# A four-layer graph attention kernel: row tiles 4-7 of layer 1 and row tile 24 of layers 2 and 3 change between gathered and all-node attention

## The chip, the cores and the metric

The kernel runs on one core of a Trainium2 chip, as one launch. The metric is the device time of a launch in microseconds, as the median of several runs; lower is better. PE is TensorE, DVE is VectorE, ACT is ScalarE, POOL is GpSimd and SP is the engine whose queue issues most plain transfers.

## What is computed

Four graph attention layers run one after the other on 4096 nodes with 256 features. Each layer is followed by a residual sum and a layer norm. All layers use one adjacency matrix; a node has itself and about 16 others as neighbours.

```
_a = bernoulli(key, 0.00390625, (4096, 4096)) | eye(4096)       # adj
...
# layer 1 (layer 0 is of the same form)
Wh = einsum('nf,hfo->hno', x, W)                      # 4 heads of 64
s1, s2 = einsum('hno,ho->hn', Wh, a1), einsum('hno,ho->hn', Wh, a2)
e = leaky_relu(s1[:, :, None] + s2[:, None, :], 0.2)
e = where(adj[None] > 0, e, NEG_BIG)
att = softmax(e, axis=-1)
h_prime = einsum('hij,hjo->hio', att, Wh)
...
x = layernorm(x + gnn(x, adj, ...))
```

Layer 2 has two heads of 128. Layer 3 has one score per pair, used once with each sign, with 256 values for each, and an ELU at its end.

## The kernel before

Nodes are taken in 32 row tiles of 128. A layer has a table of values in DRAM (`vals`): a row per node, with the head's values, each scaled, and the node's scores. For every row tile a layer computes the weighted sum over neighbours in one of two ways.

A **gathered** row tile (`RowTile`) reads only nodes that some row of the tile needs. A list of places (`idx`), made in layer 0, names for each tile 13 sets of 128 table rows; GpSimd issues an indirect transfer for each (L797), and one more set, the tile's own rows, is a plain load. The 14 sets are worked on in two halves: `half(0)` needs 6 gathers, which name only rows of tiles below 23 (`MIX`), and `half(1)` needs 7, which may name any row. In each half ACT computes exponentials set by set (L907 in layers 0 to 2, L874 in layer 3), DVE masks them (L864, L909, L876, L878), and PE multiplies by the gathered values (L928). In layers 0 and 1, three of the four heads come from ACT as the exponential of a sum of two scores (`LOGS` = 3), and the fourth from DVE as a product of two stored exponentials (`EXPS` = 1; L898 and L903). Buffers for gathered rows (`g0`, `g1`) hold four tiles.

An **all-node** row tile belongs to a group of four row tiles (`WHOLE`, by blocks of four). For each of the 32 column tiles `j` a step loads the table's values (`vw`), spreads packed mask bits into bytes (`bytes`, L660 mw), makes the weights (`pw`) and multiplies. Layers 2 and 3 do this in `whole_rows` (L1200 to L1211), where ACT and DVE make the weights and PE takes one matmul per row tile and head. Layer 1 does it in `whole_heads` (L1239 to L1290), where DVE alone makes them from exponentials held in `Sw` and `cw` (L1269), two heads in each of two passes over the 32 column tiles; PE takes eight matmuls per step, four of one form (L1272) and four of another (L1274). Every f32 matmul is two records in the trace.

Layer 0 has no all-node group. Layer 1 has block 7 (row tiles 28-31), so 28 gathered tiles. Layer 2 has blocks 3, 7 and 6, so 20. Layer 3 has blocks 7 and 6, so 24. Gathered tiles run in ascending order (`ORDER`).

The order of work is that of the program: each engine takes its own instructions in order. `steps` runs over the gathered tiles' halves; `half_with_whole` issues a half and then as many all-node steps as `whole` allows, so that all of them are spread evenly and end three tiles before the last. Finished tiles are normed (`finish`, `norm`, in groups by `GROUPS`), stored, and projected into the next layer's table by `Projection` (L677 to L742). `close` joins two layers: it loads the next layer's first tiles, projects what is left, and, from a layer that has all-node groups, runs ten steps of the next layer's groups early.

The lines that carry the two layouts are these.

```
LOGS = (3, 3, 2, 1)
EXPS = (1, 1, 0, 0)
...
WHOLE = ((), (7,), (3, 7, 6), (7, 6))
AHEAD = 10
ORDER = tuple([m for m in range(NT) if m // BT not in w] for w in WHOLE)
```

Of the kernel before, what the change touches and what calls it, by code (L numbers as in the profile page):

```python
# [37 lines left out]
F32 = mybir.dt.float32  # L38
# [3 lines left out]
I32 = mybir.dt.int32  # L42
# [8 lines left out]
P = 128  # L51
# [4 lines left out]
BT = 4  # L56
# [24 lines left out]
PAIRS = (tuple(range(1, 1 + FIRST)), tuple(range(NPAIR - FIRST)))  # L81
GROUPS = (((24, 4),), ((24, 2), (28, 1), (31, 2)), ((16, 2), (17, 1), (20, 2), (24, 1), (31, 2)), ((24, 1), (31, 4)))
LEAD = 4
# [15 lines left out]

LOGS = (3, 3, 2, 1)  # L100
EXPS = (1, 1, 0, 0)
TERMS = tuple(a + b for a, b in zip(LOGS, EXPS))
# [11 lines left out]

WHOLE = ((), (7,), (3, 7, 6), (7, 6))
AHEAD = 10
ORDER = tuple([m for m in range(NT) if m // BT not in w] for w in WHOLE)

# [8 lines left out]
def kernel(ctx: ExitStack, tc: tile.TileContext, ins: dict, out: bass.AP):  # L127
# [12 lines left out]
        "shift30": const.tile([P, 1], F32, name="shift30"),  # L140
        "shift3": const.tile([4, 4], F32, name="shift3"),
        "zero": const.tile([4, 4], F32, name="zero"),
# [14 lines left out]
    nc.vector.memset(shared["shift3"], -2.0 * KEXP)  # L157
    nc.gpsimd.affine_select(out=shared["shift3"], in_=shared["shift3"], pattern=[[1, 4]], compare_op=ALU.is_gt,
                            fill=0.0, base=0, channel_multiplier=-1)
# [24 lines left out]
class Program:  # L184
# [99 lines left out]
    def lists(self, ctx):  # L284
# [94 lines left out]
        class Block:  # L379
# [21 lines left out]
            def squeeze(self, part):  # L401
                js = slice(part * JG, (part + 1) * JG)
                src = self.mk.rearrange("p j t c -> p (j t c)").bitcast(I32) \
                    .rearrange("p (j t c) -> p j t c", j=JG, t=BT)
                w = P // 4
                for k in (4, 2, 1):
                    w //= 2
                    dst = self.bits[:, js] if k == 1 else wk.tile([P, JG, BT, w], I32, name=f"fold{k}", bufs=1)
                    nc.vector.scalar_tensor_tensor(dst, src[:, :, :, w:], k, src[:, :, :, :w],
                                                   op0=ALU.logical_shift_left, op1=ALU.bitwise_or)  # L410
                    src = dst
                if part == BT - 1:
                    rows = shared["v"][0][self.blk % 2][:N, :BW].rearrange("(j p) w -> p j w", p=P)
                    nc.sync.dma_start(out=rows, in_=self.bits.rearrange("p j t w -> p j (t w)").bitcast(F32))
                    if any(self.blk in w for w in WHOLE):
                        nc.sync.dma_start(out=shared["bitsW"][self.blk], in_=self.bits)
# [189 lines left out]
    def run(self):  # L606
# [40 lines left out]
        self.bk, self.vp, self.dp = self.pool("bk", 1), self.pool("vp", 6), self.pool("dp", 8)  # L647
        self.mwp, self.mup, self.mkp = self.pool("mwp", 2), self.pool("mup", 6), self.pool("mkp", 3)
        for n in (1, 2, 3):
# [107 lines left out]
class RowTile:  # L757
# [77 lines left out]
    def half(self, half):  # L835
# [21 lines left out]
        w = [pair[:, k, :U] for pair in pairs for k in range(2)]  # L857
        if n < 2:
            w = [w[1], w[2], w[3], w[0]]
# [20 lines left out]
        else:  # L880
# [23 lines left out]
            for h in range(A):  # L904
                for u in range(U):
                    for rows, g in parts[u]:
                        nc.scalar.activation(w[h][:, u, rows], S[:, h, rows], AF.Exp, bias=d(g, h))  # L907
                if n == 2:
                    nc.vector.scalar_tensor_tensor(w[h], w[h], LEAST, mh, op0=ALU.max, op1=ALU.mult)  # L909
                elif h % 2 == 0:  # L910
                    last = masked(pairs[h // 2])
            if n == 0:
                with self.layer.prog.tc.issue_after(last.ins):
                    nc.vector.tensor_scalar(self.kept(half), self.came(half), 0, None, op0=ALU.bitwise_or)
            turns = ((3, 0), (1, 2)) if n < 2 else ((0,), (1,))

# [38 lines left out]
class Layer:  # L955
# [3 lines left out]
    def __init__(self, prog, n):  # L959
# [5 lines left out]
        self.units = self.whole_rows() if n >= 2 else self.whole_heads()  # L965
        self.total = len(WHOLE[n]) * NT * (1 if n == 2 else 2)
        self.used = self.ahead = 0
# [200 lines left out]
    def whole_rows(self):  # L1168
        n, nc, prog, sh = self.n, self.nc, self.prog, self.shared
        H, Wd, T = HEADS[n], WIDTH[n], TERMS[n]  # L1170
        groups = [range(H)] if n < 3 else [(0,), (1,)]
        for blk in WHOLE[n]:
            tiles = range(blk * BT, (blk + 1) * BT)
            S = prog.bk.tile([P, T, BT, P], F32, name="Sw")
            for it, m in enumerate(tiles):
                nc.sync.dma_start(out=S[:, :, it, :], in_=sh["e"][n][m].partition_broadcast(P))
            bits = self.block_bits(blk)
            zs = [None] * BT
            for heads in groups:
                accs = [prog.bank(prog.pfour) for _ in range(BT)]  # L1180
                c0, c1 = heads[0] * Wd, (heads[-1] + 1) * Wd
# [10 lines left out]
                for j in range(NT):  # L1192
# [3 lines left out]
                    for h in heads:  # L1196
                        p = prog.dp.tile([P, BT, P], F32, name="pw")
                        d = sh["d"][n][:, j, h if n < 3 else 0:h + 1 if n < 3 else 1]
                        if n < 3:
                            nc.scalar.activation(p, S[:, h], AF.Exp, bias=d)  # L1200
                            nc.vector.scalar_tensor_tensor(p, p, LEAST, mj, op0=ALU.max, op1=ALU.mult)  # L1201
                        else:
                            nc.scalar.activation(p, S[:, 0], AF.Relu, bias=d)  # L1203
                            if h == 0:
# [4 lines left out]
                        c = h * Wd - c0  # L1209
                        for it in range(BT):  # L1210
                            nc.tensor.matmul(accs[it][:, c:c + Wd], p[:, it, :], v[:, c:c + Wd],  # L1211
                                             start=(j == 0 and h == heads[0]), stop=(j == NT - 1),
                                             skip_group_check=True)
                    if n == 3 and heads[0] == 0 and j == NT - 1:
                        def between(accs=accs):
                            for it in range(BT):
                                zs[it], last = self.positive(accs[it], whole=True)
                            return last
# [8 lines left out]
    def whole_heads(self):  # L1227
# [6 lines left out]
        nc.vector.tensor_scalar(c, c, HUGE, TINY, op0=ALU.min, op1=ALU.max)  # L1234
        for blk in WHOLE[n]:
            tiles = range(blk * BT, (blk + 1) * BT)
            S = prog.bk.tile([P, T, BT, P], F32, name="Sw")
            for it, m in enumerate(tiles):
                nc.sync.dma_start(out=S[:, :, it, :], in_=sh["e"][n][m].partition_broadcast(P))  # L1239


            for h in range(A):
                nc.scalar.activation(S[:, h], S[:, h], AF.Exp, scale=-1.0, bias=sh["shift30"])
                nc.vector.tensor_scalar(S[:, h], S[:, h], HUGE, None, op0=ALU.min)
            for h in range(A, T):
                nc.vector.reciprocal(S[:, h], S[:, h])
                nc.vector.tensor_scalar(S[:, h], S[:, h], LEAST, HUGE, op0=ALU.mult, op1=ALU.min)
            bits = self.block_bits(blk)
            z = prog.bk.tile([P, BT, H, Wd], F32, name="zh")
            for up, flat in TWOS:  # L1250
# [11 lines left out]
                for j in range(NT):  # L1262
# [4 lines left out]
                    for h in (up, flat):  # L1267
                        p[h] = prog.dp.tile([P, BT, P], F32, name="pw")
                        nc.vector.scalar_tensor_tensor(p[h], S[:, h], c[:, j, h:h + 1], mj, op0=ALU.max, op1=ALU.mult)  # L1269
                    how = dict(stop=j == NT - 1, skip_group_check=True)  # L1270
                    for it in range(BT):
                        nc.tensor.matmul(bu[:, it * Wd:(it + 1) * Wd], p[up][:, it, :],  # L1272
                                         v[:, up * Wd:(up + 1) * Wd], start=j == 0 and it == 0, **how)
                        nc.tensor.matmul(bf[:Wd, it * P:(it + 1) * P], v[:, flat * Wd:(flat + 1) * Wd],  # L1274
                                         p[flat][:, it, :], start=j == 0 and it == 0, **how)
                    yield
                nc.scalar.copy(z[:, :, up, :], bu[:, :BT * Wd].rearrange("p (t c) -> p t c", t=BT))
                turned = prog.bk.tile([Wd, BT, P], F32, name="turned")
                nc.scalar.copy(turned, bf[:Wd, :].rearrange("p (t i) -> p t i", t=BT))
                self.set_banks()  # L1280
                bt = prog.bank(prog.banks)
                for it in range(BT):
                    nc.tensor.transpose(bt[:, it * Wd:(it + 1) * Wd], turned[:, it, :], sh["ident"][:Wd, :Wd])
                nc.scalar.copy(z[:, :, flat, :], bt[:, :BT * Wd].rearrange("p (t c) -> p t c", t=BT))
            for it, m in enumerate(tiles):
                self.finish(m, z[:, it].rearrange("p h c -> p (h c)"), self.load_x(m), None)

    def block_bits(self, blk):
        bits = self.prog.mwp.tile([P, NT, BT, MW], I32, name="bw")
        self.nc.sync.dma_start(out=bits, in_=self.shared["bitsW"][blk])  # L1290
        return bits

    def bytes(self, bits, j):
        mj = self.prog.mup.tile([P, BT, P // 4], I32, name="mw")
        spread(self.nc, mj, bits[:, j], self.shared["pat"])
        return mj.rearrange("p t i -> p (t i)").bitcast(U8).rearrange("p (t i) -> p t i", t=BT)

# [547 lines left out]
```

## Time and profile before

| | |
|---|---|
| median of 3 runs | 2787.8 us (2785.93 to 2805.77) |
| the profiled execution's own time | 2012.93 us |
| its span | 2011.1 us |
| mean granted TensorE clock | 0.936 |
| HBM traffic | 401.51 MB read, 48.81 MB written |

The profile describes one execution, which took less time than the runs that were only timed. The span falls into stages. Up to about 100 us the first nodes are projected and the lists begun. Gathers of layer 0 start at 97.2 us, of layer 1 at 641.8, of layer 2 at 1121.0 and of layer 3 at 1533.2. Multiplication by gathered values follows its gathers by some tens of microseconds: PE works on layer 1 from about 705 to 1143 us. In a row of the groups view, the first number after the bar is the group's total busy time, the second the mean duration of one instruction in ns, and after the second bar stands the idle time of the engine ahead of the group.

### The profile page before, as it was taken

Reading aid. Unit: us, or ns where it says so; the run is one execution under the profiler, and the core shown is the slowest. Engines: PE = TensorE matmul, PEld = TensorE weight load, DVE = VectorE, ACT = ScalarE, POOL = GpSimd, SP = SyncE. Lnnn points to the kernel's source line nnn. Section 1 sums busy time; section 2 is a strip of 40 time slices with the busy share of each in tenths; the row PEclk is TensorE's granted clock in tenths of the full one; section 3 lists DMA queues with packets and bytes.
Section 4 is the critical chain, followed back from the end, with each engine's and each line's share of the span. In section 5 each row is a group of like instructions: output and inputs, shape, how many; then the busy total and the mean of one; then the engine's idle time right before and its main releaser. Section 6 shows DMA issues by size and latency. Waiting matters only on the chain.

```text
span 2011.1 us, 46792 instructions
## 1 busy us (share of the span) xinstructions
PE 1796.4 (89%) x15281; PEld 1481.6 (74%) x15281; DVE 1551.8 (77%) x5095; ACT 1498.1 (74%) x4659; POOL 1391.5 (69%) x1387
## 2 busy tenths in 40 slices
PE   5758889988999699998998989999998899899995
PEld 3537777777778589887886788898886677577773
DVE  3458988888889599988887877888876576676765
ACT  4559999898878577877666788877774687676863
POOL 0067777777777777777777677777753777767772
PEclk7758999999899799999999999999999999999998
DMA  8799999989767766666656656667666888888883
GB/s 292 227 336 325 319 298 286 293 293 296 217 170 203 200 177 190 180 182 178 179 167 183 194 158 189 199 189 203 184 187 188 248 266 247 266 251 251 258 250 105
DMA packets 291947, 453.59 MB, mean 226 GB/s; under 512 B 90246, under 2 KB 206059, under 8 KB 291692
## 3 DMA queue, kind: packets, MB, share of 16 engines
q0 software_dynamic: 74880, 227.83, 38.7%
q1 hardware_dynamic: 212194, 218.46, 35.0%
q10 hardware_dynamic: 4618, 4.20, 0.6%
q8 instruction: 123, 2.02, 0.4%
q14 instruction: 132, 1.08, 0.2%
HBM read 401.51 MB, written 48.81 MB: 224 GB/s over the span
## 4 chain that ended last, share of the span: by engine, by line
PE 46%; DMA 14%; ACT 12%; POOL 10%; DVE 9%; issue 6%; SPq 1%; DVEq 0%; ACTq 0%; POOLq 0%
PE bank L928 22%; PE bank L1211 12%; POOL G L797 10%; DMA G<-vals,idx 8%; ACT w L907 7%; PE bank L691 5%; DVE w L864 3%; DMA raw<-in_adjB_dram 2%; PE bank L1274 2%; ACT mk L399 1%; ACT pw L1200 1%; PE bank L1272 1%; DMA G<-vals 1%; PE bank L522 1%; PE bank L524 1%
## 5 line engine op out<-in xcount | busy, mean ns | idle before, releaser
L797 POOL DMA_INDIRECT G<-vals,idx x1352 | 1386.0, 1025 | 587.9 <-issue 350.0
L928 PE MATMUL bank<-G,w 128*64 128x130 f32 (+5 forms) x9156 | 920.8, 304 | 72.7 <-DVE w L864 60.7
L907 ACT ACTIVATE w<-S,G 128x64 f32<-128x64 f32 (+1 forms) x3080 | 824.3, 351 | 125.3 <-DMA G<-vals,idx 116.2
L928 PEld LDWEIGHTS bank<-G,w 128*64 128x64 f32 (+1 forms) x9156 | 741.4, 156 | 232.1 <-DVE w L864 76.5
L1211 PE MATMUL bank<-vw,pw 128*128 128x129 f32 (+1 forms) x2560 | 419.4, 322 | 13.7 <-issue 6.3
L1211 PEld LDWEIGHTS bank<-vw,pw 128*128 128x128 f32 x2560 | 375.1, 194 | 53.8 <-issue 17.7
L864 DVE SCALAR_TENSOR_TENSOR w<-w,bank 128x1024 f32<-128x1024 f32 (+1 forms) x240 | 322.7, 1345 | 10.2 <-ACT w L907 8.7
L691 PE MATMUL bank<-wext,xT 128*128 128x268 f32 (+3 forms) x640 | 185.6, 424 | 16.2 <-ACT xT L682 14.9
L874 ACT ACTIVATE w<-S,G 128x64 f32<-128x64 f32 (+1 forms) x329 | 104.1, 352 | 72.1 <-DMA G<-vals,idx 48.7
L691 PEld LDWEIGHTS bank<-wext,xT 128*128 128x128 f32 x640 | 121.4, 207 | 40.8 <-ACT xT L682 17.7
L1200 ACT ACTIVATE pw<-Sw,d 128x512 f32<-128x512 f32 x192 | 134.3, 711 | 21.0 <-PE bank L1211 12.5
L1201 DVE SCALAR_TENSOR_TENSOR pw<-pw,mw 128x512 f32<-128x512 f32 x192 | 129.5, 686 | 26.2 <-ACT pw L1200 25.1
L399 ACT ACTIVATE mk<-raw 128x1024 uint8<-128x1024 int32 x128 | 129.6, 1049 | 21.1 <-DMA raw<-in_adjB_dram 21.0
L1208 DVE TENSOR_TENSOR pw<-pw,mw 128x512 f32<-128x512 f32 x128 | 87.9, 689 | 63.1 <-ACT pw L1205 38.3
L903 DVE TENSOR_TENSOR w<-S,G 128x384 f32<-128x384 f32 x180 | 91.1, 509 | 41.8 <-DMA G<-vals,idx 36.2
L1203 ACT ACTIVATE pw<-Sw,d 128x512 f32<-128x512 f32 x128 | 89.7, 709 | 27.2 <-PE bank L928 10.4
L1272 PE MATMUL bank<-vw,pw 128*128 128x65 f32 x512 | 89.7, 258 | 17.5 <-DVE pw L1269 17.5
L1274 PE MATMUL bank<-pw,vw 128*65 128x128 f32 x512 | 99.7, 278 | 0.0
L1272 PEld LDWEIGHTS bank<-vw,pw 128*128 128x128 f32 x512 | 78.7, 195 | 26.2 <-issue 24.8
L1269 DVE SCALAR_TENSOR_TENSOR pw<-Sw,cw,mw 128x512 f32<-128x512 f32 x128 | 92.8, 740 | 0.0
L682 ACT COPY xT<-bank 128x256 f32<-128x256 f32 x128 | 45.7, 359 | 58.2 <-PE bank L677 37.9
L660 DVE TENSOR_TENSOR mw<-bw,pat 128x128 int32<-128x128 int32 x288 | 80.6, 285 | 1.6
(197 smaller groups left out, 1893.6 us busy)
## 6 DMA issues: line engine op xcount, KB each, us to landing
raw<-in_adjB_dram SPq DMA_DIRECT2D x128, 512.0 KB
G<-vals,idx POOLq DMA_INDIRECT x1352
vw<-vals SPq DMA_DIRECT2D x128, 128.5 KB
S<-edge SPq DMA_DIRECT2D x60, 256.0 KB
vw<-vals SPq DMA_DIRECT2D x96, 129.0 KB
xp<-y SPq DMA_DIRECT2D x96, 128.0 KB
y<-xp SPq DMA_DIRECT2D x96, 128.0 KB
vals<-row SPq DMA_DIRECT2D x64, 152.0 KB
```

The costliest lines, as they stand in the source:

```text
L399: nc.scalar.activation(self.mk[:, 2 * q:2 * q + 2], src, AF.Copy)
L691: nc.tensor.matmul(pp[:, :c1 - c0], self.xT[:, k, :], wext[:, k, c0:c1], start=(k == 0), stop=(k == KT - 1 and brow is None))
L797: nc.gpsimd.indirect_dma_start(out=self.row(half, k), out_offset=None, in_=self.values[:N + 1 if half else MIX * P, :].rearrange("r (k c) ...
L864: return nc.vector.scalar_tensor_tensor(pair, pair, LEAST, mh2, op0=ALU.max, op1=ALU.mult)
L874: nc.scalar.activation(w[0][:, u, rows], S[:, 0, rows], AF.Relu, bias=d(g, 0))
L907: nc.scalar.activation(w[h][:, u, rows], S[:, h, rows], AF.Exp, bias=d(g, h))
L928: nc.tensor.matmul(a, w[h][:, u, rows], b, start=half == 0 and u == 0 and (n == 3 or h == turns[0][0]), stop=half == 1, skip_group_check=True)
L1200: nc.scalar.activation(p, S[:, h], AF.Exp, bias=d)
L1201: nc.vector.scalar_tensor_tensor(p, p, LEAST, mj, op0=ALU.max, op1=ALU.mult)
L1211: nc.tensor.matmul(accs[it][:, c:c + Wd], p[:, it, :], v[:, c:c + Wd], start=(j == 0 and h == heads[0]), stop=(j == NT - 1), skip_group_ch ...
L1272: nc.tensor.matmul(bu[:, it * Wd:(it + 1) * Wd], p[up][:, it, :], v[:, up * Wd:(up + 1) * Wd], start=j == 0 and it == 0, **how)
L1274: nc.tensor.matmul(bf[:Wd, it * P:(it + 1) * P], v[:, flat * Wd:(flat + 1) * Wd], p[flat][:, it, :], start=j == 0 and it == 0, **how)
```

## The change

Layer 1 gets a second all-node group, row tiles 4-7, ahead of 28-31, so 24 tiles are gathered. Its fourth head is now an exponential of a sum from ACT as well, in gathered and all-node tiles alike (`LOGS` = 4, `EXPS` = 0). Groups are given as ranges of row tiles rather than blocks, and may have fewer than four. In layers 2 and 3 the last group becomes row tiles 25-27; row tile 24 is gathered (21 and 25 gathered tiles).

In `whole_heads` the score rows of the next group are loaded at step 8 and prepared at step 24 of the last pass over the group before, in a second `Sw` buffer. Each finish of a tile gets a turn of its own (a `yield`), with the tile's residual loaded one ahead. Gathered halves of layer 1 mask heads (0, 1) and (2, 3) in pairs after the second of a pair, and multiply in that order. The pool of mask bytes (`mup`) has five buffers instead of six, and the norm's groups follow the new last groups.

```
-GROUPS = (((24, 4),), ((24, 2), (28, 1), (31, 2)), ((16, 2), (17, 1), (20, 2), (24, 1), (31, 2)), ((24, 1), (31, 4)))
+GROUPS = (((24, 4),), ((24, 2), (28, 1), (31, 2)), ((16, 2), (17, 1), (20, 2), (25, 1), (31, 2)), ((25, 1), (28, 3), (31, 4)))
...
-LOGS = (3, 3, 2, 1)
-EXPS = (1, 1, 0, 0)
+LOGS = (3, 4, 2, 1)
+EXPS = (1, 0, 0, 0)
...
-WHOLE = ((), (7,), (3, 7, 6), (7, 6))
+WHOLE = (
+    (),
+    (range(4, 8), range(28, 32),),
+    (range(12, 16), range(28, 32), range(25, 28),),
+    (range(28, 32), range(25, 28),),
+)
...
-        self.mwp, self.mup, self.mkp = self.pool("mwp", 2), self.pool("mup", 6), self.pool("mkp", 3)
+        self.mwp, self.mup, self.mkp = self.pool("mwp", 2), self.pool("mup", 5), self.pool("mkp", 3)
...
-        if n < 2:
+        if n < 2 and A < T:
             w = [w[1], w[2], w[3], w[0]]
...
-                elif h % 2 == 0:
+                elif h % 2 == (A == T):
                     last = masked(pairs[h // 2])
...
-            turns = ((3, 0), (1, 2)) if n < 2 else ((0,), (1,))
+            turns = ((0,), (1,)) if n == 2 else ((0, 1), (2, 3)) if A == T else ((3, 0), (1, 2))
...
-        self.total = len(WHOLE[n]) * NT * (1 if n == 2 else 2)
+        self.total = len(WHOLE[n]) * NT * (1 if n == 2 else 2) + (sum(map(len, WHOLE[n])) if n < 2 else 0)
...
-        for blk in WHOLE[n]:
-            tiles = range(blk * BT, (blk + 1) * BT)
-            S = prog.bk.tile([P, T, BT, P], F32, name="Sw")
+        def scores(tiles):
+            S = prog.bk.tile([P, T, BT, P], F32, name="Sw", bufs=2)[:, :, :len(tiles)]
             for it, m in enumerate(tiles):
                 nc.sync.dma_start(out=S[:, :, it, :], in_=sh["e"][n][m].partition_broadcast(P))
+            return S
+        def floors(S):
             for h in range(A):
                 nc.scalar.activation(S[:, h], S[:, h], AF.Exp, scale=-1.0, bias=sh["shift30"])
                 nc.vector.tensor_scalar(S[:, h], S[:, h], HUGE, None, op0=ALU.min)
...
+        later = scores(WHOLE[n][0])
+        floors(later)
+        for q, tiles in enumerate(WHOLE[n]):
+            g, S = len(tiles), later
...
+                    if up == TWOS[-1][0] and q + 1 < len(WHOLE[n]):
+                        if j == JG:
+                            later = scores(WHOLE[n][q + 1])
+                        if j == 3 * JG:
+                            floors(later)
                     yield
...
+            y = self.load_x(tiles[0])
             for it, m in enumerate(tiles):
-                self.finish(m, z[:, it].rearrange("p h c -> p (h c)"), self.load_x(m), None)
+                yield
+                self.finish(m, z[:, it].rearrange("p h c -> p (h c)"), y, None)
+                if it + 1 < g:
+                    y = self.load_x(m + 1)
```

Counted over the program, from before to after: indirect gathers 1352 to 1326 (layer 1: 364 to 312; layer 2: 260 to 273; layer 3: 312 to 325); all-node steps in layer 1 64 to 128; L1211 matmuls 768 to 704 in layer 2 and 512 to 448 in layer 3; L907 exponentials 3080 to 3276; L903 and L898 together 240 to 128.

## The prediction

> **What bounds the kernel now.** I read the busy shares first, then the forty slices, then the costliest groups, then busy time by stage, then the waits and the order of time inside one stage.
>
> ```profile
> PE 1796.4 (89%) x15281; PEld 1481.6 (74%) x15281; DVE 1551.8 (77%) x5095; ACT 1498.1 (74%) x4659; POOL 1391.5 (69%) x1387
> ...
> PE   5758889988999699998998989999998899899995
> ...
> POOL 0067777777777777777777677777753777767772
> ...
> L797 POOL DMA_INDIRECT G<-vals,idx x1352 | 1386.0, 1025 | 587.9 <-issue 350.0
> L928 PE MATMUL bank<-G,w 128*64 128x130 f32 (+5 forms) x9156 | 920.8, 304 | 72.7 <-DVE w L864 60.7
> ```
>
> POOL's 7s are not slack. Of its 587.9 us idle, 350.0 are the 0.30 us between one gather and the next ("issue"). The waits of POOL leave little else: 91.7 us before the first gather, 7.5, 2.4 and 5.4 us, and this one:
>
> ```profile
> POOL G L797 <- ACT row L711: 42.2, 1, 42.2
> ```
>
> So from 132 to 1491 us gathers run back to back. Counting starts (416, 364, 260, 312 gathers for layers 0 to 3), layer 1's queue runs from 641.8 to 1121.0 us: 479.2/364 = 1.316 us a gather. Layer 2's last 236 run from 1156.3 to 1491.0: 1.418 us each. Only in layer 3 does POOL wait repeatedly, for L928 to give buffers back.
>
> Busy time by stage (span, then PE, weight load, DVE, ACT, POOL; last clock, DMA):
>
> ```profile
> 705.00:1143.00 438.00, 410.43 (x4269) 359.02 (x4264) 383.29 (x1125) 323.77 (x1241) 336.84 (x333) 0.98 0.64 181
> 1143.00:1491.00 348.00, 321.76 (x2790) 297.89 (x2789) 284.71 (x936) 273.37 (x785) 269.12 (x243) 0.97 0.66 189
> ...
> 1540.00:1960.00 420.00, 400.82 (x2135) 297.23 (x2135) 285.94 (x1020) 308.60 (x694) 304.03 (x295) 0.97 0.84 254
> ```
>
> The reader sees PE at 94, 92 and 95% in layers 1, 2 and 3. Layers 1 and 2 are held by the gather queue with PE a few per cent behind it; layer 3 is held by PE. PE's own work is read from starts, where it runs without a gap:
>
> ```profile
> 720.42 4.16 PE L928 MATMUL bank<-G,w 128*128 128x130 f32 x56
> 724.41 0.33 PE L1272 MATMUL bank<-vw,pw 128*128 128x65 f32 x2
> ...
> 725.98 4.97 PE L928 MATMUL bank<-G,w 128*128 128x130 f32 x56
> 730.78 0.33 PE L1272 MATMUL bank<-vw,pw 128*128 128x65 f32 x2
> ...
> 1159.74 8.32 PE L1211 MATMUL bank<-vw,pw 128*128 128x129 f32 x73
> ...
> 1668.42 5.36 PE L1211 MATMUL bank<-vw,pw 128*128 128x257 f32 x24
> 1673.62 4.13 PE L928 MATMUL bank<-G,w 128*128 128x257 f32 x28
> ```
>
> A layer-1 gathered half takes 724.41-720.42 = 4.0 us and the other 730.78-725.98 = 4.8: 8.8 us a row tile. Between them one all-node step (16 records) takes 725.98-724.41 = 1.57 us. L1211 costs 0.112 us a record in layer 2 (start to next start, 8.15/73) and 0.217 in layer 3 (5.20/24). Gathered tiles cost 4.7 us in layer 2 (28 records 2.13 to 2.57) and 8.75 in layer 3.
>
> **What the Trainium skill says.** "Perfetto Trace Analysis", section "Identifying the Most-Contended Engine", calls matmul busy share a bad measure because matmuls are pipelined. The trace agrees: mean L928 is 304 ns, but starts are 71 to 86 ns apart; hence prices by starts. "TensorE: Matmul & The Clock Gate", "Back-to-back issue gap", gives N/2.4+2.5 ns, 56 ns at 129 columns; the 112 ns measured for these f32 records is twice that, so the trace's price is used. The same page, "HAM oscillation", says idle gaps bring the clock down: from 680 to 700 us PE was busy 4.96 of 20 us at a clock of 0.51. A steadier PE could regain a little.
>
> **The change, part by part.**
>
> *Layer 1, tiles 4-7 to all nodes.* Gathers: 4 x 13 = 52 fewer, 52 x 1.316 = 68 us less POOL. PE: minus 4 x 8.8 = 35, plus 64 steps x 1.57 = 100: **+65 us**. DVE: two L1269 (92.8/128 = 0.725 effective) and one mask spread (80.6/288 = 0.28) a step, 64 x 1.73 = +111; four gathered tiles less, each four L864 (322.7/60 = 5.4) and unpacking (about 1.1), -26. ACT: 4 x 42 exponentials less at the effective 0.27 us (824.3/3080), -45. SP: 64 more L1258 loads of 130 KB, four score rows and one mask block in place of four tiles' loads and 52 gathers of about 137 KB; bytes balance within 2 MB at a DMA share of 0.64. One more mask block (256 KB) is stored in layer 0, under 1 us at its 300 GB/s, beside other work. The eight yields and the scores fetched eight steps into a pass hide behind matmuls; were that cover gone, one late score row costs about 4 us (Sw waits elsewhere reach 4.5).
>
> *Fourth head from ScalarE.* In 24 tiles, 14 more exponentials each: 24 x 14 x 0.27 = +91 us ACT. DVE loses L903 (three) and L898 (one), about 1.8 us a tile: -51 over the old 28. Layer-1 totals on the 705-1143 base: PE 410+65 = 475, DVE 383+111-26-51 = 417, ACT 324-45+91 = 370 and ten small ones more, POOL 312 x 1.316 = 411. ACT and DVE stay under PE, so I cost the head itself at nothing; the cover is PE's 475. Without it DVE at 417 would be late next. L903 also held DVE's queue while gathers landed (28.8 us between 900 and 1100), blocking L1269 behind it; that wait goes with a queue that no longer bounds.
>
> PE thus becomes layer 1's bound. It starts at 705 either way, so the stage ends no earlier than 705+475 = 1180, against 1143: **+37** with no idle left, +65 if all 27.6 us of idle stay. I take **+45**. POOL will now wait for buffers, as in layer 3, and does not carry its lead into layer 2: layer 2's second-half gathers need every layer-1 result.
>
> *Layer 2, tile 24 gathered.* POOL +13 x 1.418 = +18. PE minus 128 records x 0.112 = 14.3, plus 4.7 = -10. ACT: 28 exponentials more (+8), 64 all-node ones shorter by a quarter (0.711 us to about 0.60: -7). DVE: 64 x (0.14+0.07) less, 4 more maskings of 0.75: -10. The gather queue bounds here: **+12** (0 to +18; PE pulls the other way).
>
> *Boundary to layer 3.* The 42.2 us wait is for rows of tiles below 23, the only ones that first halves gather. Tile 22 is now third from last instead of second, so the wait can shrink by a tile's pace, up to 17 us. But PE is 47 of 49 us busy there with projections: **-7** (-17 to 0).
>
> *Layer 3, tile 24 gathered.* PE minus 128 x 0.217 = 27.8, plus 8.75: -19. POOL's 13 more gathers (16 us) fit into its waits for buffers. **-20** rounded (-24 to -8, less if POOL's waits run out).
>
> Small edits together (five mask buffers, two score buffers, group sizes of the norm, order of turns): hidden while PE has a queue of ready weights; bounded at -5 to +10, taken as 0.
>
> Sum: +45+12-7-20 = **+30 us** on the profiled execution's 2012.9 us (span 2011.1 and 1.8 around it): 2043, +1.5%. The median of the runs shown is 2787.8, 1.385 times the profiled one, and nothing in the trace accounts for 775 us. I carry the ratio over: 2787.8 x 1.015 = **2829**. Carried as plain microseconds it would be 2818.
>
> **The rivals.** *Gathers are what is longer outside the profile.* If the missing 775 us lie in the 1352 gathers, each costs 0.57 us more. Then POOL bounds layer 1 before and after (312 x 1.89 = 590, over PE's 475), and the change saves 52 x 1.89 = 98 there and gives back 26 x 1.9 = 50 in layers 2 and 3, with some 10 us won at the boundary: 2787.8-48-10 = **2730**, faster. It decides from about 1.40 us a gather in layer 1, where the 364 old ones are longer by 364 x 0.08 = 30 us, the loss forecast above. For it: an unbroken queue over 1359 us is where a hidden cost would add up. Against: 1.316 in the profile.
>
> *PE's idle is given back everywhere.* Layer 1 takes only +37, layer 2's extra gathers hide in the boundary (+18-17) and layer 3 gives -24: +14, or **2807**, within 1%. For it: PE was 100% busy from 720 to 880 us beside a DVE at 96%. Against: DVE at 417 of 475 leaves little freedom.
>
> *The edit doesn't do what it says*, because ACT in order, with 56 exponentials a tile, delays both paths: layer 1 at +65, boundary nothing, total about +55, **2864**. Against: 370 of 475.
>
> **How the numbers follow.** About 1% (28 us) is what a measurement of this kernel tells from no change: its runs spread over 0.7%. Likeliest case 0.40 (own range 2807 to 2850), ACT rival 0.09, even rival 0.21, gather rival 0.30. Slower by over 1% takes the ACT rival and most of the likeliest case: 0.44. Within 1%: the even rival and the edges of the others, 0.26. Faster: 0.30, nearly all of the gather rival. The range goes from that rival's 2725 to 2880, a layer 1 with all its idle kept and some layer-2 gathers uncovered.
>
> **What would show it.** Right: POOL gaps of over 1 us before gathers in layer 1, waiting for L928; PE near 100% to the end of that stage; its end near 1185; L1211 about 45 us less busy (64/768 of its 184 us in layer 2, 64/512 of its 235 in layer 3). Wrong: gathers in layer 1 still 0.30 us apart; PE's starts for an all-node step under 1.57 us; the wait at the layer-3 boundary unchanged; or a span shorter while the timed runs are longer, which would put the answer into the 775 us.

## The result and the profile after

The kernel after takes 2796.6 us (median of 20 runs), the kernel before 2795.2 beside it: ratio 1.0011 [0.9992, 1.0029]. The forecast was 2829 us, +1.5%. The time lies in the forecast's range, but the change that was forecast is not there.

The program turned out to run at two levels whatever the change: the kernel before took 2771 to 2810 us in the timed runs, about 2014 us in some later sets of runs and in its first profile, and on one and the same chip both 2015 and 2750. Below, the *long* and the *short* times; ratios are only ever taken inside one set. The profile after is one of the long time (2791.3 us).

Page of the kernel after: busy shares, slices, groups.

```profile
PE 2117.5 (76%) x15721; PEld 1687.1 (60%) x15721; DVE 1585.9 (57%) x5173; ACT 1553.1 (56%) x4852; POOL 1342.4 (48%) x1361
...
PE   5547767666677677688888887768888879998986
...
POOL 0254533434434444644444442446556455666664
PEclk7657777777776778799989998879999989998998
...
L802 POOL DMA_INDIRECT G<-vals,idx x1326 | 1337.1, 1008 | 1418.9 <-issue 614.5
L933 PE MATMUL bank<-G,w 128*64 128x130 f32 (+4 forms) x8820 | 1112.9, 330 | 373.1 <-issue 340.9
```

A gather takes no longer than before (1008 ns against 1025), yet POOL idles 1419 us. PE idles 373 us ahead of gathered matmuls, 341 of it by "issue": it waited for nothing that the trace shows. Before, that row had 72.7 us idle and named a DVE operation. Layers 1, 2 and 3 by stage, columns as in the prediction:

```profile
1050.00:1678.00 628.00, 518.13 (x4649) 450.95 (x4648) 405.45 (x1086) 343.33 (x1308) 299.40 (x296) 0.91 0.47 129
1740.00:2209.00 469.00, 372.41 (x2797) 319.35 (x2793) 291.55 (x998) 283.50 (x852) 265.77 (x255) 0.88 0.53 145
2260.00:2761.00 501.00, 444.88 (x2211) 312.06 (x2211) 300.47 (x1110) 321.54 (x743) 330.85 (x324) 0.93 0.77 231
```

PE stands at 83, 79 and 89%, the DMA share at 0.47 in layer 1: nothing is full. The timelines of PE and of POOL in layer 0 of this kernel show how:

```profile
642.38 0.27 PE L481 MATMUL bank<-past,kinds 128*4 128x128 f16 x1 [1.05 <-issue]
643.78 0.26 PE L485 MATMUL bank<-past,kinds 128*32 128x128 f16 x1 [1.14 <-issue]
644.52 0.26 PE L485 MATMUL bank<-upto,kinds 128*32 128x128 f16 x1 [0.47 <-issue]
646.65 0.26 PE L485 MATMUL bank<-past,kinds 128*32 128x128 f16 x1 [1.87 <-issue]
648.77 0.27 PE L485 MATMUL bank<-upto,kinds 128*32 128x128 f16 x1 [1.85 <-issue]
```

```profile
643.79 0.94 POOL L802 DMA_INDIRECT G<-vals,idx  x1 [0.30 <-issue]
645.04 0.95 POOL L802 DMA_INDIRECT G<-vals,idx  x1 [0.31 <-issue]
```

Matmuls start 1.40, 0.74, 2.13, 2.12 us apart: one, two or three times about 0.71 us. I call these **steps**, and sum the distances between successive matmul starts that lie within 5% of one to six times 0.707 us. The trace after holds 505 us of them, the first profile of before 37, the level below which the count says nothing.

### The profile page after: what moved, and what is told of

Its sections match the earlier page's. It is cut to its first block, busy times and chain, and to the rows that moved or that the text cites. A ratio compares the mean times of both kernels' runs of the same rounds, so it can differ in the third digit from the quotient of the medians.

```text
span 2789.6 us, 48067 instructions
## 1 busy us (share of the span) xinstructions
PE 2117.5 (76%) x15721; PEld 1687.1 (60%) x15721; DVE 1585.9 (57%) x5173; ACT 1553.1 (56%) x4852; POOL 1342.4 (48%) x1361
## 5 line engine op out<-in xcount | busy, mean ns | idle before, releaser
L802 POOL DMA_INDIRECT G<-vals,idx x1326 | 1337.1, 1008 | 1418.9 <-issue 614.5
L933 PE MATMUL bank<-G,w 128*64 128x130 f32 (+4 forms) x8820 | 1112.9, 330 | 373.1 <-issue 340.9
L933 PEld LDWEIGHTS bank<-G,w 128*64 128x64 f32 (+1 forms) x8820 | 846.9, 173 | 614.6 <-issue 512.2
L912 ACT ACTIVATE w<-S,G 128x64 f32<-128x64 f32 (+1 forms) x3276 | 874.5, 351 | 216.5 <-PE bank L933 70.4
L1216 PE MATMUL bank<-vw,pw 128*128 128x129 f32 (+1 forms) x2304 | 399.0, 329 | 30.8 <-issue 25.8
L1216 PEld LDWEIGHTS bank<-vw,pw 128*128 128x128 f32 x2304 | 349.6, 199 | 77.0 <-issue 44.2
L1280 DVE SCALAR_TENSOR_TENSOR pw<-Sw,cw,mw 128x512 f32<-128x512 f32 x256 | 184.6, 745 | 124.7 <-remote 81.4
L1285 PE MATMUL bank<-pw,vw 128*65 128x128 f32 x1024 | 201.0, 280 | 11.8 <-issue 11.5
L1205 ACT ACTIVATE pw<-Sw,d 128x512 f32<-128x512 f32 (+1 forms) x192 | 128.1, 678 | 134.1 <-remote 64.4
L1206 DVE SCALAR_TENSOR_TENSOR pw<-pw,mw 128x512 f32<-128x512 f32 (+1 forms) x192 | 121.8, 643 | 118.6 <-ACT pw L1205 83.9
L1283 PE MATMUL bank<-vw,pw 128*128 128x65 f32 x1024 | 176.5, 257 | 7.5 <-issue 7.3
L879 ACT ACTIVATE w<-S,G 128x64 f32<-128x64 f32 (+1 forms) x343 | 111.6, 354 | 96.0 <-DMA G<-vals,idx 64.5
L1213 DVE TENSOR_TENSOR pw<-pw,mw 128x512 f32<-128x512 f32 (+1 forms) x128 | 78.9, 621 | 78.1 <-ACT pw L1212 24.5
L1285 PEld LDWEIGHTS bank<-pw,vw 128*65 128x65 f32 x1024 | 106.1, 143 | 16.8 <-issue 16.7
```

Source lines behind the costliest of these rows:

```text
L802: nc.gpsimd.indirect_dma_start(out=self.row(half, k), out_offset=None, in_=self.values[:N + 1 if half else MIX * P, :].rearrange("r (k c) ...
L933: nc.tensor.matmul(a, w[h][:, u, rows], b, start=half == 0 and u == 0 and (n == 3 or h == turns[0][0]), stop=half == 1, skip_group_check=True)
L1205: nc.scalar.activation(p, S[:, h, :g], AF.Exp, bias=d)
```

## The experiments

**The parts alone, at the long times** (before 2788.9 us). e1_before is the kernel before, unchanged. The others are the kernel after with parts put back. The small edits of the change (mask bytes, score buffers, turns of the finishes) stay in all three; no run has them alone:

```
e2_layer1:   WHOLE[2], WHOLE[3] and GROUPS as before
e3_layers23: LOGS = (3, 3, 2, 1); EXPS = (1, 1, 0, 0); WHOLE[1] = (range(28, 32),)
e4_head:     WHOLE and GROUPS as before (the fourth head and the small edits change)
```

> The kernel before, unchanged, profiled a second time. Theory 'PE is held up at issue': the profiled execution of before that the prediction was read from (2012.9 us) was not like the timed runs (2795 us); this one takes 2780 to 2810 us, and its trace shows what the trace of after shows, PE matmuls starting in steps of about 0.7 us with 'issue' before them, some 300 to 400 such starts instead of 13, and gathers that are no longer back to back in layer 0. Theory 'gathers are longer outside the profile': 2780 to 2810 us too, but with POOL's gathers at 1.6 us or more each and PE waiting for them. If it takes about 2013 us again, the two kernels do differ in the profiled state and the timed runs are the odd ones.

Measured 0.9993 [0.9973, 1.0012], with 486 us of steps in its trace: they were there before the change, and the timed runs are like this trace, not like the first profile.

> Layer 1's part alone (tiles 4-7 to all nodes, fourth head from ScalarE); layers 2 and 3 as before. Prediction's mechanism (PE's work in layer 1 grows by 65 us and is on the path): slower by 45 us or more, ratio 1.016 or above. Gather rival (52 gathers fewer at 1.9 us): faster by about 98 us, ratio 0.965. 'Held up at issue' (neither PE's streaming nor the gathers set the time): within 0.6%, perhaps 10 to 28 us slower for the 592 more PE matmul records.

> Layers 2 and 3's part alone (tile 24 gathered, last group of three tiles); layer 1 as before. Prediction's mechanism (+12 in layer 2, -7 at the boundary, -20 in layer 3): faster by about 15 us, ratio 0.995. Gather rival: slower by about 40 to 50 us, ratio 1.016. 'Held up at issue': faster by 5 to 25 us, as PE's work falls by 29 us in stages where PE is still the busiest.

> The fourth head of layer 1 from ScalarE alone; all row tiles and groups as before. Prediction: nothing (ratio within 0.3% of 1), the work moves from DVE to ACT beside PE. If DVE's products that wait for a whole half's gathers hold up the queue behind them: faster, up to 1%. If ACT's exponentials are on the path of the halves: slower by up to 2%.

Measured: layer 1 0.9953 [0.9931, 0.9975], or -13 us; layers 2 and 3 1.0031 [1.0014, 1.0048], +9 us; the head alone 0.9961 [0.9941, 0.9981], -11 us. So "no change" is two parts of opposite signs, each with the sign opposite to its term in the forecast, and the head, costed at nothing, is most of the gain. Their sum, -4 us, agrees with the +3 of the whole change within the intervals. Moving row tiles 4-7 is worth the difference of e2 and e4, -2 us, which is within the noise of both.

**Do the gathers make the steps?** Theory S: at the long times, PE's instructions come in steps while GpSimd issues gathers. e6_plain_before (and e5_plain_after on the kernel after) has no gathers; it leaves out the list of places, so that the weights multiply rows of other nodes:

```
-            nc.gpsimd.indirect_dma_start(out=self.row(half, k), ..., in_offset=...)
+            t = ((22, 21, 11), (27, 31, 23))[half][pos % 3]
+            nc.sync.dma_start(out=self.row(half, k), in_=self.values[t * P:(t + 1) * P, :ROW[n]])
```

e7_pool_plain has `nc.gpsimd` for `nc.sync` there; e8_extra adds gathers of a quarter row in layer 1:

```
+            if n == 1 and pos % 4 == 1:
+                c = PITCH[n] // STRIDE
+                junk = prog.ep.tile([P, c], F32, name="junk", bufs=4)
+                nc.gpsimd.indirect_dma_start(out=junk, ..., in_offset=...idx[:, m, 1:2]...)
```

> The kernel before with each of its 1352 indirect gathers replaced by a plain load of 128 consecutive table rows, issued by SP, of the same size into the same buffer. The attention weights then multiply other nodes' rows, so the output differs; every other instruction stays. Theory S (PE's instructions come in steps of about 0.7 us only while GpSimd issues indirect gathers; some 480 us of PE's time in the kernel before): the steps vanish from the trace and the time falls by 300 us or more, to 2000 to 2480. Rival B (the steps belong to the execution as a whole, whoever moves the rows): some 300 gaps of 0.7 us or more ahead of matmuls stay, and the time stays above 2650.

> The kernel after with the same replacement (1326 gathers become plain loads issued by SP; the output differs in the same way). Theory S: with the steps gone, what is left of the change is PE's own work, +65 us in layer 1 against -10 and -19 in layers 2 and 3: 20 to 45 us slower than e6_plain_before, most of it in layer 1. Rival B: the two stand to each other as the kernels after and before do, within 0.3%.

> The kernel before with 84 more gathers in layer 1 (three a row tile, a quarter row wide, into a tile that nobody reads). Nothing waits for them but GpSimd's own queue. Theory S, at layer 1's 117 us of steps over 364 gathers = 0.32 us a gather: +27 us, between +15 and +55. Rival D (GpSimd's queue bounds layer 1, as the profile of before had it): 84 x 1.25 = +105 us. Rival E (GpSimd's waits, 222 us in layer 1, take them in): 0 to +10.

> The kernel before with the same plain loads as e6_plain_before, but issued by GpSimd. Theory S in a wider form (GpSimd making descriptors for any transfer disturbs PE): steps of 0.7 us stay, time within 150 us of the kernel before. In its narrow form (indirect transfers alone disturb): no steps, time as e6_plain_before within 60 us.

All four ran at the short time (before 2013.9 us), where there are no steps, so none could decide between S and its rivals. Ratios: e6 0.9854 [0.9800, 0.9908], e5 0.9921 [0.9903, 0.9939], e7 0.9652 [0.9618, 0.9685], e8 1.0503 [1.0473, 1.0533]. The fall of 300 us that S asked for did not come: without indirect gathers the kernel before falls by 1.5 (e6) to 3.5% (e7). e5 is 7 us over e6 by the medians and 13 by the ratios, not 20 to 45. But e8 is informative: 84 gathers cost 101 us, 1.20 us each, nearly their pitch of 1.25 us in the queue. That is rival D: at the short time GpSimd's queue does bound layer 1, as the first profile said. Repeats (f3_plain_before, g1_plain_before; f4_extra, g2_extra) again fell at the short time and gave 0.9860 and 0.9871, 1.0519 and 1.0505.

**The prediction's own ground.** f1_after is the kernel after, f2_layer1 is e2_layer1, at the short time (before 2015.5 us). These expectations take the level for a property of the chip; h1_mixed showed later that it isn't.

> The kernel after, unchanged, once more. The kernel before takes about 2790 us on one chip and about 2014 us on another (that of the profile of before). Where it takes 2014, PE's instructions don't come in steps of 0.7 us, and the prediction's sum can be seen by itself: +30 us (+11 to +55), 2044 us, with PE at 95% or more in layer 1 and GpSimd waiting there. Where it takes 2790: within 0.3% of it, as measured.

> The layer-1 part alone (row tiles 4-7 to all nodes and the fourth head from ACT; layers 2 and 3 as before), once more. On the chip where the kernel before takes 2014 us: the prediction's term for layer 1, +45 us (+37 to +65). Rival (GpSimd's queue gives back more than PE takes, as e8_extra's +101 us for 84 gathers suggests): 0 to -25 us. Where it takes 2790: 0.5% less, as measured.

f1: 1.0032 [1.0021, 1.0044], +6 us; f2: 1.0010 [1.0000, 1.0020], +2 us, far from the forecast's +37 to +65 and next to the upper end of the rival's 0 to -25. So the sum of +30 fails at the level where its profile was taken, too. Windows of the kernel before in its first profile:

```profile
680.00:700.00 20.00, 4.96 (x26) 4.99 (x26) 8.81 (x13) 5.09 (x14) 15.43 (x16) 0.51 0.58 168
700.00:720.00 20.00, 17.45 (x181) 16.00 (x180) 16.07 (x30) 15.59 (x60) 15.43 (x16) 0.98 0.54 156
...
1040.00:1080.00 40.00, 34.76 (x371) 29.69 (x369) 33.02 (x89) 26.97 (x105) 30.85 (x31) 1.00 0.62 175
1080.00:1100.00 20.00, 13.11 (x103) 10.90 (x102) 14.15 (x70) 13.09 (x50) 15.43 (x16) 0.83 0.65 194
```

and of f1_after:

```profile
680.00:700.00 20.00, 11.50 (x99) 11.21 (x99) 10.02 (x17) 8.85 (x33) 13.02 (x15) 0.82 0.69 202
700.00:720.00 20.00, 20.00 (x205) 19.30 (x205) 17.79 (x38) 17.83 (x70) 15.44 (x16) 0.92 0.59 160
...
1040.00:1080.00 40.00, 40.00 (x428) 37.45 (x428) 36.50 (x93) 28.53 (x112) 26.13 (x26) 1.00 0.62 173
1080.00:1100.00 20.00, 20.00 (x217) 18.64 (x215) 18.98 (x50) 17.86 (x64) 15.71 (x15) 1.00 0.63 177
```

PE (first number after the span) is full from 700 us to the layer's end. Summed over such windows from 641 to 1160 us, its idle time falls from 48 to 13 us; 8 of these 35 us lie before 720 us, 27 after. PE's longest waits between 600 and 1200 us, before:

```profile
PE bank L928 <- DVE w L864: 19.8, 17, 5.4
PE bank L1272 <- DVE pw L1269: 17.5, 1, 17.5
```

and in f1_after:

```profile
PE bank L933 <- DVE w L869: 15.0, 8, 8.5
```

The 17.5 us are a single wait, from 678 to 695 us, and not one for gathers: the first all-node step waits for its weights. They need the score rows of tiles 28-31, which SP asks for between 666 and 684 us. The kernel after begins with tiles 4-7, whose rows are asked for at 606 us, and this wait is gone. j1_l3 below, with layer 1's row tiles as before, has it again (16.5 us).

Nor does PE's work grow by 65 us. From layer 1's first gather to layer 2's first second-half gather, the first that needs every result of layer 1, PE is busy 466 us before (641.8:1156.3), 513 in f1 (642.1:1169.9) and 517 in f2 (638.7:1165.4). That is +47 and +51; by start distances without the idle time, f2's all-node steps take 95 us more and its gathered matmuls 41 less. Of f2's 51 us, 39 fit into idle time (48 before, 10 left) and 12 lengthen the stretch.

**The steps, layer by layer.** h1_mixed is the kernel before with SP's plain loads in layers 0 and 2, e8's extra gathers in layer 1, and layer 3 unchanged:

```
+            if n in (0, 2):
+                nc.sync.dma_start(...)              # as e6_plain_before
+            else:
                 nc.gpsimd.indirect_dma_start(...)
+                if n == 1 and pos % 4 == 1: ...     # as e8_extra
```

> The kernel before with plain loads issued by SP in place of the gathers of layers 0 and 2 (their output differs), 84 more narrow gathers in layer 1 that nobody reads, and layer 3 unchanged. Read layer by layer where the kernel before takes 2790 us, by the time that matmuls spend in steps of 0.7 us (kernel before: layer 0 246 us, layer 1 117, layer 2 69, layer 3 21). Theory S (gathers cause the steps): layers 0 and 2 below 20 us each, layer 1 120 to 170, layer 3 as before; total below 2600. Rival B (the steps come whoever moves the rows): layers 0 and 2 keep over half of theirs, total above 2650. Where before takes 2014: no steps in any layer, +60 to +105 us from layer 1's queue.

It ran at the long time: 2415.2 us beside 2750.1, 0.8793 [0.8690, 0.8895]. Steps by layer (cut where each layer's gathers start, layer 0 from the span's start), and the same for other traces of the long time. The entries are good to about 5 us; the first profile of before, at the short time, has 17, 8, 12 and 0.

| us of steps | layer 0 | layer 1 | layer 2 | layer 3 |
|---|---|---|---|---|
| e1_before | 268 | 126 | 70 | 22 |
| h1_mixed | 47 | 186 | 1 | 25 |
| after | 299 | 75 | 67 | 63 |
| e2_layer1 | 292 | 77 | 62 | 41 |
| e4_head | 312 | 112 | 54 | 35 |
| e3_layers23 | 262 | 118 | 71 | 68 |

The groups view agrees. PE's gathered matmuls of e1_before in layer 0 (150 to 1010 us) and layer 2 (1720 to 2200):

```profile
L928 PE MATMUL bank<-G,w 128*64 128x130 f32 (+1 forms) x3237 | 424.2, 344 | 213.7 <-issue 191.9 <-DVE w L864 14.0 <-ACT w L907 4.3
...
L928 PE MATMUL bank<-G,w 128*64 128x129 f32 (+3 forms) x1170 | 135.0, 300 | 47.7 <-issue 43.7 <-DMA G<-vals,idx 3.4 <-ACT w L907 0.2
```

and of h1_mixed in layers 0 (150 to 698 us), 1 (750 to 1470) and 2 (1500 to 1890):

```profile
L938 PE MATMUL bank<-G,w 128*64 128x130 f32 (+1 forms) x3233 | 336.9, 322 | 56.1 <-DVE w L874 55.3 <-PE bank L504 0.5
...
L938 PE MATMUL bank<-G,w 128*64 128x130 f32 (+1 forms) x2828 | 334.2, 309 | 146.6 <-issue 130.5 <-ACT w L917 11.7 <-DMA G<-vals,idx 2.4
...
L938 PE MATMUL bank<-G,w 128*64 128x129 f32 (+3 forms) x1400 | 130.7, 285 | 0.8 <-DVE w L874 0.8
```

In the two layers without gathers "issue" vanishes and the idle time falls to 56 and 1 us, near the 43 and 0 of the first profile; in the one with gathers both stay. Rival B falls. My limits were too narrow: layer 0 keeps 47 us (under 20 expected), layer 1 has 186 (120 to 170). Layer 0, from the span's start to layer 1's first gather, shrinks from 1012 to 699 us.

A second sign goes with the first. The long traces hold fewer semaphore events (the records that name what a wait was for), so the name "issue" alone proves little; but in h1_mixed the loss, too, is confined to the layers with gathers. By layer it holds 16,164, 4,713, 11,648 and 4,320 events, e1_before 8,440, 5,058, 5,444 and 3,987, the first profile 16,670, 12,490, 10,845 and 11,247. The distances between starts don't depend on these events.

What a gather brings is not constant: e1_before's steps are 0.64, 0.35, 0.27 and 0.07 us a gather in layers 0 to 3. And steps are not the whole of the stretch. They are 486 of the 761 us between e1_before's span and the first profile's; in layer 0 PE is also busy longer (580 us in 150:1010 against 447 in 150:640), at a clock of 0.71 instead of 0.94.

The same run prices a gather: layer 1's queue, first gather to last, grows from 677 us (e1) to 775, 98/84 = 1.17 us for each extra one, though POOL waits for 213 us in that layer beyond the 0.30 us between gathers. At the long time these waits don't take gathers in. The two traces are of different sets (before 2788.9 and 2750.1), so this price is rough.

**What is left: layers 2 and 3.** i1_l12 is the kernel after with layer 3 as before; j1_l3 has only layer 3 changed; i2_pool0 has e7's plain loads in layer 0 alone, and 48 extra gathers in layer 3 (`n == 3 and pos % 6 == 1`).

```
i1_l12: WHOLE[3] = (range(28, 32), range(24, 28),); GROUPS[3] = ((24, 1), (31, 4))
j1_l3:  e3_layers23 with WHOLE[2] and GROUPS[2] as before
```

> The kernel after with layer 3 as before (row tiles 24-27 as its last all-node group; layers 1 and 2 as after). Where the kernel before takes some 2780 us: if layer 3's 13 added gathers are what the layer-2-and-3 part loses (theory S: its steps went from 21 to 61 us), 0.5 to 0.9% below the kernel before; if layer 2's are, within 0.2% of it. Where the kernel before takes some 2014: +0.2 to +0.6%, as the gathers added in layer 2 bound it there.

> The kernel before with plain loads in place of layer 0's gathers, issued by GpSimd (the output differs), and 48 more narrow gathers in layer 3 that nobody reads. Where the kernel before takes some 2780 us, by steps of 0.7 us: layer 0 keeps over 120 us if any descriptors made by GpSimd bring them, under 40 if only indirect transfers do (SP's plain loads left 36). Layer 3: theory S 21 + 48 x 0.32 = 36 us or more, rival (its steps have another cause) below 25. Where the kernel before takes some 2014: no steps in layer 0; total within 60 us of the kernel before.

> The kernel after with layers 1 and 2 as before: only row tile 24 of layer 3 moves from all-node to gathered. Where the kernel before takes some 2780 us: theory S (the added gathers bring steps, 21 to 61 us, over the 19 us of matmuls saved) +0.3 to +0.9%; rival (the loss of e3_layers23 is layer 2's) within 0.2%. Where it takes some 2014: -0.1 to -0.3%, by the difference of f1_after (+0.32%) and i1_l12 (+0.49%); the prediction's term was -20 us, -1.0%.

All ran at the short time (before 2012.8, for j1_l3 2013.6): i1 1.0049 [1.0030, 1.0067], j1 0.9960 [0.9942, 0.9978], i2 1.0270 [1.0239, 1.0301] without steps, like its forecast for that case. Layer 2 alone is then i1 less f2, +0.4% or +8 us (about 4 either way); layer 3 alone, with the small edits, is -8 us, a little more than j1's -0.1 to -0.3%. Which of the two costs 9 us at the long time was not measured by a run. In the traces it is layer 3: from its first gather to the end it takes 512 us in e1_before and e2_layer1 and 519 in e4_head, 543 in e3_layers23 and 535 after.

No version was seen to beat both kernels at both levels: e2_layer1 gains 0.5% at the long and nothing at the short time; j1_l3 gains 0.4% at the short time and wasn't run at the long one.

## Why the prediction was wrong, step by step

**What bounds the kernel.** Right for the execution profiled: in layer 1 an added gather costs its pitch (e8). That execution was not one of those timed.

**Layer 1, +45: the step that failed.** Measured +2 at the short time (f2) and -13 at the long (e2). PE is the layer's bound after the change, as forecast, and GpSimd waits. Wrong was "It starts at 705 either way, so ... +37 with no idle left", in two terms. The window 705 to 1143 saw 27.6 us of idle; the layer's idle, from its first gather to its last result, was 48 us, of which 10 to 15 are left; the wait of 17.5 us for the first all-node weights is not there when tiles 4-7 come first. And PE's work grew by 47 to 51 us, not 65. What is left lengthens the layer by 12 to 13 us, not 45. That f2 as a whole loses only 2 is not traced further: layer 3, unchanged in it, takes 469 us in f2's trace, 478 in that of before. How f2's +2 divides between row tiles and head is open as well, since the head alone was not run at the short time. The cross-check was at hand: 52 gathers at the queue's price (68 us in the prediction, 52 x 1.20 = 62 by e8) are about what PE was priced to add (65) and above what it does add, so one bound takes the other's place at nearly the same height.

At the long time the queue gives back 52 x 1.17 = 61 us, an estimate from h1, against about 50 of matmuls; that these two balance there was not tried by a run of its own. Steps in layer 1 fall from 126 to 77 us (e1 to e2), and the clock there rises. Windows of the two, from layer 1's first gather to layer 2's:

```profile
1012.00:1719.00 707.00, 548.82 (x4538) 457.98 (x4538) 411.21 (x1224) 346.42 (x1329) 359.23 (x365) 0.84 0.44 124
```

```profile
1016.00:1703.00 687.00, 568.23 (x5180) 496.04 (x5178) 454.45 (x1287) 393.81 (x1504) 313.76 (x312) 0.92 0.46 128
```

642 more matmul records cost PE only 19 us of busy time, at a clock of 0.92 instead of 0.84, in a stage 20 us shorter than e1's. Against e3_layers23, whose layer 1 also keeps its row tiles and head, it is 8 us shorter (687 and 695).

**Fourth head, 0.** -11 us at the long time, with the small edits. The traces don't place this gain: layer 1 goes from 707 to 691 us (e1 to e4), but e3, without the new head, has 695, and 13 of the 16 us lie between layer 1's last gather and layer 2's first. The forecast had L903 blocking DVE's queue and called that wait worthless because another bound would take over; whether that wait is what the head saves was not tried.

**Layer 2, +12, and the boundary, -7.** Right: +8 together by i1 and f2. In f1's trace the last 249 gathers run from 1169.9 to 1515.0 us, +10 on the old 334.7, and the wait before layer 3 is 33.9 instead of 42.2 us.

**Layer 3, -20.** Sign right at the short time, size not: -8 (j1). Sums of start distances over layer 3 give 236 us for L1211 before and 214 in j1 (L1216 there), -22 where 27.8 was taken, and +10 for gathered matmuls where 8.75 was taken. Without the idle time in them these are -27 and +11, close to the prices; but PE's idle time in the layer doesn't shrink with the records (19 us before, 25 in j1). "POOL's 13 more gathers fit into its waits" failed at the long time: the layer's steps are 63 to 68 us with the change to layer 3 and 22 to 41 without.

**The ratio of 1.385, carried over.** It assumes that all stages stretch alike. They don't: layer 0 goes from 642 to 1012 us, layer 3 from 478 to 512, and h1 shows that in layers 0 and 2 the stretch goes when the gathers go. The warning "nothing in the trace accounts for 775 us" was the place to give up the sum.

**The rivals.** The gather rival had the right suspect and the wrong mechanism: gathers don't last longer, they slow PE, and GpSimd then waits for PE. Its 98 us for layer 1 assumed that PE at full speed stays below the queue. The even rival (2807, within 1%) came closest. At the short time its reason holds in layer 1, where idle time is given back. At the long times, where the medians were taken, its being right is luck: there two parts of opposite sign cancel.

## What to carry over

Compare the profiled execution's time with the timed median first; where they differ by a third, no sum made from that profile forecasts the median, and a second profile is worth more than any price in the first. Where work moves from a full queue to an engine with idle time, price the move at both bounds over the whole layer, first wait to last result, since the lower bound's idle is filled before the layer grows. A change that measures as nothing can be parts of opposite sign: run them alone.

## What the runs showed of the hardware

- At the long times PE's instructions start in steps of 0.71, 1.42 and 2.13 us while GpSimd issues indirect gathers: 0.7 us of steps for each of the 84 gathers added in h1_mixed (layer 1: 186 less 126 us, over 84), and 47 and 1 us in the two layers whose rows SP loads, where e1_before has 268 and 70. By what path GpSimd holds PE up, no run shows. The long traces hold fewer semaphore events (24,063 in that of after against 51,537 in the first profile), so some of the "issue" in them may be a release that wasn't recorded; in h1_mixed the loss comes and goes with the gathers, as the steps do.
- The level belongs neither to the kernel nor to the chip: the chip that gave 2015 us for the kernel before beside f1_after gave 2750 beside h1_mixed, within half an hour. Which of the chip's cores ran is not on record. What sets the level stays open. So does whether plain transfers issued by GpSimd bring steps, as e7 and i2 fell at the short time.
- At the short time a plain load takes GpSimd 539 ns (e7) where an indirect one takes 1025, and the kernel, with other rows loaded, gains 3.5%.
